# Moving four of eleven blocks of sequence 1's integer layer between the matmuls of sequence 0's down projection

## The chip, the cores and the metric

The kernel runs on one core of one Trainium2 chip. The metric is the device time of one execution in microseconds: 904.87 us, the median of three runs (904.53 to 905.12). Matmuls run on TensorE (PE in the profile), evictions and elementwise work on VectorE (DVE), ScalarE (ACT) and GpSimd (POOL); SyncE (SP) issues nearly all DMAs.

## The reference, cut to what matters

Two sequences of 512 tokens with 512 features pass four layers, each of which adds a normalised result to `x`: a state-space layer, a feed-forward layer with 4-bit integer weights ("the integer layer"), an attention over 16 head positions, and a feed-forward layer with experts ("the latent layer").

```python
x = x + _layernorm(_L0_attn_ref(_layernorm(x), ...))
x = x + _layernorm(_L0_ffn_ref(_layernorm(x), ...))    # the integer layer
x = x + _layernorm(_L1_attn_ref(_layernorm(x), ...))
x = x + _layernorm(_L1_ffn_ref(_layernorm(x), ...))
# in _L0_ffn_ref, Wg, Wu and Wd being dequantized 4-bit weights:
gate = x2 @ Wg
up = x2 @ Wu
inter = gate * jax.nn.sigmoid(gate) * up
out = (inter @ Wd).astype(jnp.float16)
```

A weight is (q - z - 1) times a scale that holds for a group of 128 rows. The inner size is 1376, cut into eleven blocks of up to 128 (`IC`); the input size of 512 is four groups.

## The kernel before, in words

The program is traced by Python generators. A stream yields after each step of matmuls; `run` (L1230) then serves one waiting request for transposes (`answer`, L1222), advances the clock of ticks (`tick`, L707) and lets every job that is due trace its next instructions. `pin` (L396) fixes the order of tracing as the order of PE, ACT, DVE and POOL. DMAs on SP are not pinned: the framework orders them, and SP issues them one after the other. `answer` serves a request no sooner than three ticks after the last one.

The state-space layer of both sequences comes first. Beside the scans of sequence 1, sequence 0 already gets its gate and up products of the integer layer, with weights that have their scales in them; its intermediate rows `it0_0` to `it0_10` then lie in SBUF.

After the scans (L1202 on) `outs` (L1285) runs 32 matmuls of sequence 1's output projection, and then sequence 0's down projection: eleven blocks times four token tiles, 44 matmuls into the four banks `fo0`. Its weights `wd0` come through the pool `wst`, three buffers, which also serves all gate and up weights. Beside that run the jobs that unpack the down weights (`words_jobs`), and `normed_job` (L1240) for each of the four token tiles of sequence 1: it normalises, asks for four transposes, and splits the result into a high and a low part, `hhl`, in float32r.

Then `run(gptq(1))` (L1635) does sequence 1's integer layer. Here the weights are plain integers (`wgi_d`), and the scales are applied when a result is evicted. `group` (L1429) multiplies one block by one group of 128 rows: two matmuls, for the high and the low part, into one of three PSUM banks (`bank`, L1214). `evict` (L1410) scales the first of a pair of groups on ACT (L1415) and adds the second to it on DVE (L1419); POOL adds the two pairs (L1423), and `inter` applies Silu on ACT and the product on DVE. A step of the stream has two groups, so a block takes four steps for gate (`fg`) and up (`fu`) together. From the third block on, each such step is followed by one down matmul (`fo`, L1394) of the block two before (`LAG = 2`), and eight down matmuls end it: 88 steps in all. The first block's weights are asked for at the start of the layer.

Beside this stream a job traces `chain(0)` (L1629) for sequence 0: eviction of `fo0` (`ffn_out`), the norm of the integer layer (`gptq_norm`), a norm with four sets of transposes (`layer_T`, tiles `tp_a`), the projection `pqkv`, the attention on DVE and ACT, and a second norm with transposes (`tp_l`). All these transposes go through one PSUM bank (`tbank`, L1209). `chain(0)` counts in the same ticks as the stream.

What follows is not pinned: `chain(1)` does the same for sequence 1 (and its `tp_a`, `pqkv` and `tp_l`), and `latent(0)` and `latent(1)` fill TensorE to the end, with `pfe`, `pup`, `pr`, `plg` and `pd`.

Of the kernel before, what the change touches and what calls it, by code (L numbers as in the profile page):

```python
# [9 lines left out]
F32 = mybir.dt.float32  # L10
F16 = mybir.dt.float16
F32R = mybir.dt.float32r
# [45 lines left out]
def tile_sandwich(  # L58
# [358 lines left out]
    with ExitStack() as mamba:  # L417
# [783 lines left out]
        ps_x = pool(ctx, "px", 1, PSUM)  # L1201
        ps_tp = pool(ctx, "ptp", 1, PSUM)  # L1202
        hlp = pool(ctx, "hl", side="right")
        hhl = [hlp.tile([P, KH, S], F32R, name=f"h{nm}1") for nm in ("hi", "lo")]

        def obank(name):
# [13 lines left out]
        answered = [0]  # L1220

        def answer():  # L1222
            if now[0] < answered[0] + 3:
                return
            answered[0] = now[0]
            fn, then = asks.pop(0)
            fn()
            spawn(then, 1)

        def run(stream, every=lambda: True):  # L1230
            for _ in stream:
# [2 lines left out]
                tick()  # L1234
                pin()

        with ExitStack() as p3:
            dq = pool(p3, "dq2", 1)

            def normed_job(i, ps):  # L1240

                name = f"mo1_{i}"
                o = new_u(f"o1_{i}")
                nc.scalar.copy(o, ps)
                yield 3
                mv = moments([o], name)
                rs = rstd(mv, name, 1)
                yield 2
                nm = minus_mean(mv, rs, name, 1)
                yield 1  # L1250
                apply(o, o, rs, nm, 0)
                yield 2
                nc.vector.tensor_add(xs(1)[i], xs(1)[i], o)
                name = f"f1_{i}"
                mv = moments([xs(1)[i]], name)
                rs = rstd(mv, name, 1)
                yield 2
                nm = minus_mean(mv, rs, name, 1)
                yield 1
                xn = jrow(f"xn_{name}")  # L1260
                apply(xn, xs(1)[i], rs, nm, 0)
                yield 2
                tps = []

                def turn():
                    tp = bank(f"tp_f1_{i}").rearrange("p (k t) -> p k t", k=KH)
                    for kc in range(KH):
                        nc.tensor.transpose(tp[:, kc, :], xn[:, ts(kc, P)], ident)
                    tps.append(tp)

                def split():
                    hi, lo = (t_[:, :, ts(i, P)] for t_ in hhl)
                    nc.scalar.copy(hi, tps[0])
                    yield 1
                    nc.vector.tensor_sub(lo, tps[0], hi.bitcast(F32))

                asks.append((turn, split()))

            def words_jobs():
                yield from down_words(0, dq, down[0])  # L1280
                yield from down_words(1, dq, down[1])
                yield 20
                yield from head_sums(dq)

            def outs():  # L1285
                po = [obank(f"po1_{i}") for i in range(TB)]
                for j in range(NCH // 2):
                    w = wo_pair(1, 0, j)
                    tiles = [(e, i) for e in range(2) for i in range(TB)]
                    for e, i in sorted(tiles, key=lambda ei: ei[j == NCH // 2 - 1]):  # L1290
                        c = 2 * j + e
                        nc.tensor.matmul(  # L1292
                            po[i], g[1][c][:, ts(i, P)], w[:, e, :],
                            start=(c == 0), stop=(c == NCH - 1),
                        )
                        yield
                        if c == NCH - 1:
                            spawn(normed_job(i, po[i]), 1)
                for i, m in enumerate(IC):
                    j, e = divmod(i, 2)  # L1300
                    if not e:
                        w = wst.tile([P, 2, H], F32, tag="w4", name=f"wd0_{j}")
                        n = len(IC[i : i + 2])
                        nc.sync.dma_start(
                            out=w[:m, :n],
                            in_=wd_d[i * P : i * P + n * m].rearrange("(k p) h -> p k h", p=m),
                        )
                    for t in range(TB):
                        if not i:
                            fo0.append(obank(f"fo0_{t}"))  # L1310
                        nc.tensor.matmul(  # L1311
                            fo0[t], its[i][:m, ts(t, P)], w[:m, e],
                            start=(i == 0), stop=(i == len(IC) - 1),
                        )
                        yield

            fo0 = []
            spawn(words_jobs(), 1)
            run(outs())
            while jobs or asks:  # L1320
                if asks:
                    answer()
                tick()
            pin()
# [17 lines left out]
        nc.sync.dma_start(out=t_[:rows], in_=src)  # L1342
        return t_

    gus16 = wdp.tile([P, 2, len(IC), KH], F16, name="gus16")
    nc.sync.dma_start(out=gus16, in_=gu_scales)
    gus = wdp.tile([P, 2, len(IC), KH], F32, name="gus")
    nc.vector.tensor_copy(gus, gus16)
    gam = wdp.tile([P, H], F32, name="gam")
    bet = wdp.tile([P, H], F32, name="bet")  # L1350

    def layer_T(b, name, ask):
# [13 lines left out]
        for i in range(TB):  # L1366
            while i >= 2 and i - 2 not in done_tp:
                yield 1
            xn = nrow(f"xn_{name}{b}_{i}")
            apply(xn, xs(b)[i], rs, nm, i)  # L1370
            yield 1

            def turn(i=i, xn=xn):
                tp = done_tp[i] = tbank(f"tp_{name}{b}_{i}").rearrange("p (k t) -> p k t", k=KH)
                for kc in range(KH):
                    nc.tensor.transpose(tp[:, kc, :], xn[:, ts(kc, P)], ident)  # L1376

            def out(i=i):
                nc.scalar.copy(hT[:, :, ts(i, P)], done_tp[i])
                done.append(i)  # L1380
                yield 1

            ask(turn, out())
# [2 lines left out]

    def gptq(b):
        fo = [obank(f"fo{b}_{t}") for t in range(TB)]
        its, ups, parts = {}, {}, {}

        def down(i, w):
            m = IC[i]
            for t in range(TB):
                nc.tensor.matmul(  # L1394
                    fo[t], its[i][:m, ts(t, P)], w[:m],
                    start=(i == 0), stop=(i == len(IC) - 1),
                )
                yield
# [2 lines left out]
            m = IC[i]  # L1401
            return w2(wd_d[i * P : i * P + m, :], f"wd{b}_{i}", m)

        def inter(i):
            m, it, up = IC[i], its[i], ups[i]
            nc.scalar.activation(it[:m], it[:m], AF.Silu)
            yield 1
            nc.vector.tensor_mul(it[:m], it[:m], up[:m])

        def evict(a, i, k, ps):  # L1410
            m = IC[i]
            sc = gus[:m, a, i, k : k + 1]
            if k % 2 == 0:
                t_ = parts[a, i, k] = row(f"p{'gu'[a]}{b}_{i}_{k}")
                nc.scalar.activation(t_[:m], ps[:m], AF.Copy, scale=sc)  # L1415
                return
            t_ = parts[a, i, k - 1]
            yield 1
            nc.vector.scalar_tensor_tensor(t_[:m], ps[:m], sc, t_[:m], ALU.mult, ALU.add)  # L1419
            if k == KH - 1:  # L1420
                yield 1
                p0 = parts[a, i, 0]
                nc.gpsimd.tensor_add(p0[:m], p0[:m], t_[:m])  # L1423
                (ups if a else its)[i] = p0
                if a:
                    yield 2
                    yield from inter(i)

        def group(a, i, k, w):  # L1429
            e, m = i % 2, IC[i]  # L1430
            ps = bank(f"f{'gu'[a]}{b}_{i}_{k}")
            for n, part in enumerate(hhl):
                nc.tensor.matmul(  # L1433
                    ps[:m], w[:, k, e * P : e * P + m].bitcast(F32R), part[:, k, :],
                    start=(n == 0), stop=(n == 1),
                )
            spawn(evict(a, i, k, ps), 1)

        LAG = 2
        wd = {}  # L1440
        for i in range(len(IC)):
            if i % 2 == 0:
                ws = gu_weights(b, i // 2)
            wd[i] = wd_load(i)
            dn = down(i - LAG, wd[i - LAG]) if i >= LAG else iter(())
            for a in range(2):
                for k in range(0, KH, 2):
                    group(a, i, k, ws[a])
                    group(a, i, k + 1, ws[a])
                    yield  # L1450
                    for _ in dn:
                        yield
                        break
        for i in range(len(IC) - LAG, len(IC)):
            yield from down(i, wd[i])
        fos[b] = fo

    fos = {}
# [255 lines left out]
```

## Time and profile before

| | |
|---|---|
| median of three runs | 904.87 us (904.53 to 905.12) |
| profiled execution, its own time | 905.83 us |
| span of the profile, first to last instruction | 904.1 us |
| mean granted TensorE clock over the span | 0.971 |
| sequence 0's down projection begins | 599.55 us |
| integer layer of sequence 1 | 639.54 to 735.41 us |
| `latent(0)` begins | 735.41 us |
| last matmul ends, about | 894.25 us |

In a profile's list by time, a row gives the start and the length in us, engine, line and operation, `out<-in`, the shapes and the count, and in brackets how long the engine had idled before it and what released it. In a table of busy time by stage, a row gives the stretch and its length, the busy time and count for PE, PEld (the loading of weights into TensorE), DVE, ACT and POOL, the granted clock of TensorE, the share of the DMA engines that was busy, and GB/s. In the groups, a row gives the line, engine and operation, the shapes and the count, then the busy time, the mean length in ns, and the idle time before with its releaser. A matmul of float32 shows as two passes, one of float32r as one.

### The profile page before, as it was taken

The page shows a single profiled execution, that of the slowest core. Times are in us where ns is not written, and L with a number is a line of the kernel's source. Part 1 is how long each engine was busy: PE and PEld are TensorE (multiplying, and loading weights), DVE is VectorE, ACT ScalarE, POOL GpSimd, SP SyncE. Part 2 cuts the span into 40 slices and gives each one's busy share as a digit, 9 for nine tenths or more (in the row PEclk, how much of TensorE's full clock was granted, in tenths as well). Part 3 has the DMA queues.
Part 4 walks back from the last instruction along what each step waited for, and adds up shares of the span by engine and source line. Part 5 has one row for each costly group of instructions (what it writes and reads, how often), then busy time and mean ns, then how long its engine had stood idle before and what let it go on. Part 6 is the DMA issues. An engine that isn't in the chain of part 4 may idle for free. (4 is left out here: it accounts for less than half of the span.)

```text
span 904.1 us, 7390 instructions
## 1 busy us (share of the span) xinstructions
PE 826.8 (91%) x2188; PEld 382.6 (42%) x2188; DVE 717.8 (79%) x835; ACT 441.1 (49%) x682; POOL 507.0 (56%) x354
## 2 busy tenths in 40 slices
PE   6889979797999989779999998999989999999995
PEld 3434434233454434334444442344456545545442
DVE  5869999999999999999999998763576964444226
ACT  3359875657666755566566653031455444400110
POOL 6767796778778878876787878540233410011001
PEclk9998999898999999979999999799999999999998
DMA  6759211110001765300011112572322331101001
GB/s 214 283 205 381 80 55 56 47 55 31 24 1 61 259 252 196 107 0 24 24 46 47 32 33 78 187 252 81 93 71 82 95 106 47 46 12 58 24 0 47
DMA packets 47418, 85.76 MB, mean 95 GB/s; under 512 B 8302, under 2 KB 22489, under 8 KB 47378
## 3 DMA queue, kind: packets, MB, share of 16 engines
q1 hardware_dynamic: 45106, 79.30, 25.8%
q0 software_dynamic: 1984, 5.47, 1.7%
q10 hardware_dynamic: 288, 0.52, 0.2%
q8 instruction: 17, 0.28, 0.1%
q14 instruction: 23, 0.19, 0.1%
HBM read 68.40 MB, written 16.88 MB: 94 GB/s over the span
## 5 line engine op out<-in xcount | busy, mean ns | idle before, releaser
L1100 POOL TENSOR_TENSOR bx<-bx,C 128x1024 f32<-128x1024 f32 x128 | 302.3, 2362 | 101.9 <-DVE bx L1094 79.7
L1094 DVE TENSOR_TENSOR_SCAN bx<-da,bx 128x1024 f32<-128x1024 f32 x128 | 292.3, 2283 | 0.5 <-ACT da L1074 0.4
L1122 PE MATMUL py<-bx,ident 128*128 128x512 f32 x480 | 234.9, 619 | 27.9 <-POOL bx L1100 24.3
L1074 ACT ACTIVATE da<-dt,A 128x511 f32<-128x511 f32 x256 | 176.9, 692 | 149.4 <-DVE bx L1094 144.7
L1122 PEld LDWEIGHTS py<-bx,ident 128*128 128x128 f32 x480 | 91.6, 196 | 153.1 <-issue 97.1
L1090 DVE TENSOR_TENSOR bx<-du,B 128x1024 f32<-128x1024 f32 x127 | 153.4, 1209 | 2.3 <-DMA B<-scr 0.3
L130 POOL TENSOR_TENSOR rs_lo<-ve_lo,mhalf 128x1 f32<-128x1 f32 x8 | 7.1, 882 | 91.8 <-DVE ve_lo L128 91.8
L745 PE MATMUL pg<-xT,w_g 128*128 128x512 f32 x114 | 55.8, 620 | 1.1 <-ACT dt L563 1.1
L1554 PE MATMUL pup<-hT_l,wup 128*128 128x512 f32 x128 | 56.2, 593 | 0.0
L1618 PE MATMUL pd<-wdn,hid 128*128 128x512 f32 x128 | 55.5, 594 | 0.0
L1423 POOL TENSOR_TENSOR pg<-pg,pg 128x512 f32<-128x512 f32 (+1 forms) x11 | 15.3, 1392 | 59.2 <-DVE pg L1419 59.2
L1394 PE MATMUL fo<-wd,pg 128*128 128x512 f32 (+1 forms) x88 | 44.2, 593 | 0.1
L1014 PE MATMUL fg<-hT_f,wg 128*128 128x512 f32 (+1 forms) x88 | 42.5, 594 | 0.0
L1014 PE MATMUL fu<-hT_f,wu 128*128 128x512 f32 (+1 forms) x88 | 40.4, 594 | 1.4 <-ACT dt L563 1.4
L475 DVE SCALAR_TENSOR_TENSOR u<-px,ch,u 128x511 f32<-128x511 f32 (+2 forms) x48 | 35.9, 747 | 6.5 <-ACT u L468 5.4
L1311 PE MATMUL fo<-wd,it 128*128 128x512 f32 (+1 forms) x88 | 38.6, 592 | 0.0
L1618 PEld LDWEIGHTS pd<-wdn,hid 128*128 128x128 f32 x128 | 24.6, 192 | 31.2 <-issue 30.7
L1571 DVE TENSOR_TENSOR hid<-hid 128x512 f32<-128x512 f32 x16 | 11.0, 688 | 32.0 <-ACT hid L1570 31.8
L1554 PEld LDWEIGHTS pup<-hT_l,wup 128*128 128x128 f32 x128 | 23.9, 190 | 28.2 <-issue 28.2
L745 PEld LDWEIGHTS pg<-xT,w_g 128*128 128x128 f32 x114 | 22.1, 198 | 31.6 <-issue 28.7
L1419 DVE SCALAR_TENSOR_TENSOR pg<-fg,gus,pg 128x512 f32<-128x512 f32 (+1 forms) x22 | 16.4, 744 | 21.5 <-ACT pg L1415 21.5
L615 PE MATMUL px<-xT,w_x 128*128 128x512 f32 x64 | 31.7, 645 | 0.7 <-ACT xT L595 0.7
(253 smaller groups left out, 1256.5 us busy)
## 6 DMA issues: line engine op xcount, KB each, us to landing
wo<-in_W_outT SPq DMA_DIRECT2D x20, 512.0 KB
B<-scr SPq DMA_DIRECT2D x16, 512.0 KB
C<-scr SPq DMA_DIRECT2D x16, 512.0 KB
w_x<-in_W_in SPq DMA_DIRECT2D x8, 512.0 KB
wgi_d<-q_gu SPq DMA_DIRECT2D x16, 256.0 KB
wgu_d<-w_gu POOLq DMA_DIRECT2D x16, 256.0 KB, 2.6
w_g<-in_W_in SPq DMA_DIRECT2D x8, 512.0 KB
wup<-in_up_w SPq DMA_DIRECT2D x8, 512.0 KB
```

Of the source, the lines that this page charges most:

```text
L475: nc.vector.scalar_tensor_tensor(uc[:, s:], ps[:, : S - s], ch[:, c, KCONV - 1 - s : KCONV - s], uc[:, s:], ALU.mult, ALU.add,)
L745: nc.tensor.matmul(ps, w[:, k, ts(e, P)], xT[b][:, k, :], start=(k == 0), stop=(k == KH - 1))
L1014: nc.tensor.matmul(ps[:m], wt[j][a][:, kc, e * P : e * P + m], hT[:, kc, :], start=(kc == 0), stop=(kc == KH - 1),)
L1074: nc.scalar.activation(das[s % 2][:, i, 1:], st["dt", b, c][:, 1:], AF.Exp, scale=A[:, c, n : n + 1])
L1090: nc.vector.tensor_mul(bx, st["du"].unsqueeze(1).to_broadcast([P, NG, S]), Bbs[b][gi])
L1094: nc.vector.tensor_tensor_scan(flat, das[s % 2].rearrange("p n t -> p (n t)"), flat, 0.0, ALU.mult, ALU.add)
L1100: nc.gpsimd.tensor_mul(bxs[s], bxs[s], Cbs[b][s % NGI])
L1122: nc.tensor.matmul(st["y"], ident, bx[:, i, :], start=False, stop=last)
L1311: nc.tensor.matmul(fo0[t], its[i][:m, ts(t, P)], w[:m, e], start=(i == 0), stop=(i == len(IC) - 1),)
L1394: nc.tensor.matmul(fo[t], its[i][:m, ts(t, P)], w[:m], start=(i == 0), stop=(i == len(IC) - 1),)
L1554: nc.tensor.matmul(ps, w[:, kc, ts(e, P)], src[kc], start=(kc == 0), stop=(kc == KH - 1))
L1618: nc.tensor.matmul(pd, hid[kc][:, ts(i, P)], wdn[kc], start=(kc == 0), stop=(kc == INT // P - 1),)
```

## The change

Blocks 0 to 3 (`MIX = 4`) of sequence 1's integer layer move into the stretch of sequence 0's down projection. `mixed` runs down matmuls until all four tiles of `hhl` are split, and then one step of two groups for every two down matmuls. The gate rows of the four blocks get their own pool (`it1`), other partial rows reuse `g1` tiles. `wd0` gets its own three buffers, and the scales `gus` are loaded earlier. All jobs are drained before `gptq` begins.

`gptq` has the other seven blocks: four steps of groups alone (`FIRST = 4`), then one step of groups and one down matmul by turns (`GD = 2`). `downs` now starts with block 0, without a lag. When the groups are at their end, their turns pass as ticks without a matmul. `answer` may serve a request at every tick, and of sequence 0's sets of transposes every second one uses `bank` instead of `tbank`.

```diff
         hlp = pool(ctx, "hl", side="right")
+        gus16 = hlp.tile([P, 2, len(IC), KH], F16, name="gus16")
+        nc.sync.dma_start(out=gus16, in_=gu_scales)
+        gus = hlp.tile([P, 2, len(IC), KH], F32, name="gus")
+        nc.vector.tensor_copy(gus, gus16)
...
-            if now[0] < answered[0] + 3:
+            if now[0] < answered[0] + 1:
                 return
...
+        def int_groups(row, a, i, ws):
+
+            for k in range(0, KH, 2):
+                group(a, i, k, ws[a], row)
+                group(a, i, k + 1, ws[a], row)
+                yield
+
+        def int_layer(row, i0, i1):
+
+            for i in range(i0, i1):
+                if i % 2 == 0 or i == i0:
+                    int_ws[0] = gu_weights(1, i // 2)
+                for a in range(2):
+                    yield from int_groups(row, a, i, int_ws[0])
+
+        its1, ups, parts, int_ws, ready = {}, {}, {}, [None], set()
+        MIX, GD, FIRST = 4, 2, 4
+
+        itp = pool(ctx, "it1", MIX, side="right")
         with ExitStack() as p3:
             dq = pool(p3, "dq2", 1)
+            wdq = pool(p3, "wd0", 3, side="right")
...
+            def down0():
                 for i, m in enumerate(IC):
                     j, e = divmod(i, 2)
                     if not e:
-                        w = wst.tile([P, 2, H], F32, tag="w4", name=f"wd0_{j}")
+                        w = wdq.tile([P, 2, H], F32, tag="wd0", name=f"wd0_{j}")
...
+            def row1(a, i, k):
+                if (a, k) == (0, 0):
+                    return itp.tile([P, S], F32, tag="it", name=f"it1_{i}")
+                row1s[0] += 1
+                return g1_tile(F32, row1s[0] % NCH, f"p{'gu'[a]}1_{i}_{k}")
+
+            row1s = [-1]
+
+            def mixed():
+                fo = down0()
+                while split_count[0] < TB:
+                    next(fo)
+                    yield
+                gu = int_layer(row1, 0, MIX)
+                ends, n = {}, 0
+                while not all(ends.get(k) for k in (gu, fo)):
+                    k = fo if n % 3 else gu
+                    ends[k] = next(k, True)
+                    n += 1
+                    yield
...
             run(outs())
+            run(mixed())
             while jobs or asks:
                 if asks:
                     answer()
                 tick()
...
-                tp = done_tp[i] = tbank(f"tp_{name}{b}_{i}").rearrange("p (k t) -> p k t", k=KH)
+                tp = done_tp[i] = (tbank if b or i % 2 == 0 else bank)(f"tp_{name}{b}_{i}").rearrange("p (k t) -> p k t", k=KH)
...
+        def downs():
+            wd = {0: wd_load(0), 1: wd_load(1)}
+            for i in range(len(IC)):
+                if i + 2 < len(IC):
+                    wd[i + 2] = wd_load(i + 2)
+                while i not in ready:
+                    yield "wait"
+                yield from down(i, wd.pop(i))
+
+        gu, dn = int_layer(row_, MIX, len(IC)), downs()
+        for _ in range(FIRST):
+            next(gu)
+            yield
+        n, gu_end, dn_end = 0, None, None
+        while not (gu_end and dn_end):
+            if n % GD == 0:
+                gu_end = next(gu, True)
+            else:
+                dn_end = next(dn, True)
+                if dn_end == "wait":
+                    gu_end, dn_end = next(gu, True), None
+            n += 1
+            yield
```

`group`, `evict` and `inter` move out of `gptq` to be used by both stretches, with the tile that receives a partial result given by `row`; they trace the same instructions as before.

More of the change, by code (lines that the diff above doesn't have):

```diff
@@ L1235, in run, with inter, evict, group @@
                 pin()
+        def inter(i):
+            m, it, up = IC[i], its1[i], ups.pop(i)
+            nc.scalar.activation(it[:m], it[:m], AF.Silu)
+            yield 1
+            nc.vector.tensor_mul(it[:m], it[:m], up[:m])
+            ready.add(i)
+        def evict(a, i, k, ps, row):
+            m = IC[i]
+            sc = gus[:m, a, i, k : k + 1]
+            if k % 2 == 0:
+                t_ = parts[a, i, k] = row(a, i, k)
+                nc.scalar.activation(t_[:m], ps[:m], AF.Copy, scale=sc)
+                return
+            t_ = parts[a, i, k - 1]
+            yield 1
+            nc.vector.scalar_tensor_tensor(t_[:m], ps[:m], sc, t_[:m], ALU.mult, ALU.add)
+            if k == KH - 1:
+                yield 1
+                p0 = parts[a, i, 0]
+                nc.gpsimd.tensor_add(p0[:m], p0[:m], t_[:m])
+                (ups if a else its1)[i] = p0
+                if a:
+                    yield 2
+                    yield from inter(i)
+        def group(a, i, k, w, row):
+            e, m = i % 2, IC[i]
+            ps = bank(f"f{'gu'[a]}1_{i}_{k}")
+            for n, part in enumerate(hhl):
+                nc.tensor.matmul(
+                    ps[:m], w[:, k, e * P : e * P + m].bitcast(F32R), part[:, k, :],
+                    start=(n == 0), stop=(n == 1),
+                )
+            spawn(evict(a, i, k, ps, row), 1)
+        def int_groups(row, a, i, ws):
[12 more added lines that the diff above has]
+        itp = pool(ctx, "it1", MIX, side="right")
         with ExitStack() as p3:
             dq = pool(p3, "dq2", 1)
+            wdq = pool(p3, "wd0", 3, side="right")
             def normed_job(i, ps):
@@ L1275, in split @@
                     nc.vector.tensor_sub(lo, tps[0], hi.bitcast(F32))
+                    split_count[0] += 1
                 asks.append((turn, split()))
@@ L1315, in outs @@
                         yield
-            fo0 = []
+            def row1(a, i, k):
[16 more added lines that the diff above has]
+                    yield
+            fo0, split_count = [], [0]
             spawn(words_jobs(), 1)
             run(outs())
+            run(mixed())
             while jobs or asks:
@@ L1343, in w2 @@
         return t_
[L1345 to L1348, printed above, removed]
     gam = wdp.tile([P, H], F32, name="gam")
@@ L1388, in gptq @@
         fo = [obank(f"fo{b}_{t}") for t in range(TB)]
-        its, ups, parts = {}, {}, {}
         def down(i, w):
@@ L1394, in down @@
                 nc.tensor.matmul(
-                    fo[t], its[i][:m, ts(t, P)], w[:m],
+                    fo[t], its1[i][:m, ts(t, P)], w[:m],
                     start=(i == 0), stop=(i == len(IC) - 1),
@@ L1402, in wd_load @@
             return w2(wd_d[i * P : i * P + m, :], f"wd{b}_{i}", m)
[L1404 to L1453, printed above, removed]
@@ L1454, in gptq, with row_ @@
-        for i in range(len(IC) - LAG, len(IC)):
-            yield from down(i, wd[i])
+        def row_(a, i, k):
+            return row(f"p{'gu'[a]}1_{i}_{k}")
+        def downs():
[7 more added lines that the diff above has]
+        gu, dn = int_layer(row_, MIX, len(IC)), downs()
```

## The prediction

> **What bounds the kernel now.** I read the page first, then the matmuls in order of time from 599 us, busy time by stage, the waits, and the groups by form. The page says that TensorE is the busy engine to the end, and that from slice 24 it seldom rests:
>
> ```profile
> PE 826.8 (91%) x2188; PEld 382.6 (42%) x2188; DVE 717.8 (79%) x835; ACT 441.1 (49%) x682; POOL 507.0 (56%) x354
> ...
> PE   6889979797999989779999998999989999999995
> ```
>
> So a change that only reorders matmuls can win only what TensorE idles in the stretch concerned. That stretch begins with sequence 0's down projection at 599.55. Timeline of TensorE:
>
> ```profile
> 599.98 7.89 PE L1311 MATMUL fo<-wd,it 128*128 128x512 f32 x18
> 607.71 0.60 PE L1268 MATMUL tp_f<-ident,xn_f 128*128 128x128 f32 x4
> ...
> 617.19 22.48 PE L1311 MATMUL fo<-wd,it 128*128 128x512 f32 x52
> ...
> 735.41 7.13 PE L1554 MATMUL pfe<-hT_l,wfe 128*128 128x512 f32 x16
> ```
>
> 52 passes fill 617.19 to 639.54: 0.43 us a pass, 0.86 a down matmul (two passes), nothing lost. In the integer layer a *unit* is two groups, four matmuls. Unit plus down matmul recur every 1.79 us (690.30, 692.09, 693.88), so a unit is 0.93. A set of four transposes takes 0.44 (610.72 to the next matmul at 611.16), the attention projection 3.5 (685.34 to 688.83). Busy time by stage gives the elapsed times:
>
> ```profile
> 639.54:651.79 12.25, 10.62 (x38) 5.78 (x36) 9.93 (x23) 9.12 (x14) 4.93 (x4) 1.00 0.38 103
> 651.79:671.33 19.54, 18.02 (x57) 10.15 (x57) 18.43 (x31) 7.42 (x12) 7.50 (x6) 1.00 0.31 98
> 671.33:685.34 14.01, 13.15 (x53) 8.26 (x53) 6.11 (x9) 9.62 (x16) 3.83 (x3) 1.00 0.21 57
> 685.34:735.41 50.07, 49.30 (x185) 29.66 (x183) 37.73 (x65) 28.12 (x44) 17.53 (x13) 1.00 0.32 96
> ```
>
> Elapsed minus work is what TensorE lost. First row: 9 units, 8.4 of work, lost 3.85. Second: 9 units and 10 downs, 17.0, lost 2.5. Third: 6 units, 6 downs, four sets of transposes, 12.5, lost 1.5. Fourth: 20 units, 28 downs, projection, four sets, 48.0, lost 2.0. Together 9.85 us, and no more can be won here. The cause stands in the groups by form (DVE's and ACT's evictions, 0.74 and 0.69 us each) and in the wait of a unit: it starts when an eviction frees its PSUM bank.
>
> ```profile
> L1419 DVE SCALAR_TENSOR_TENSOR pg<-fg,gus,pg 128x512 f32<-128x512 f32 x20 | 14.9, 744 | 21.5 <-ACT pg L1415 21.5
> ...
> L1415 ACT ACTIVATE pg<-fg,gus 128x512 f32<-128x512 f32 x20 | 13.7, 687 | 18.2 <-PE fg L1433 18.2
> ...
> 665.70 0.50 PE L1433 MATMUL fu<-hhi,wu 128*128 128x512 f32 x1 [0.81 <-DVE pg L1419]
> ```
>
> **The change part by part.** The order on each compute engine is the order of tracing, so I count ticks (one per step of the matmul stream). The count is tested on before: it puts the first tp_a set behind 10 downs and the first tp_l set behind 35, as the trace has them.
>
> *Scales.* One load and a cast (0.20) move from 619.84 to ahead of the nibbles at 570.39. Were the load late, the down words slip; their cover is the wd0 load issued at 591.66 for a use at 599.55. I take 0 (bounds 0 and +2); past the cover each us costs one. On SP, the load waited 10.8 us for py; that wait goes, and nothing behind it was late.
>
> *Loads.* wd0 gets three buffers of its own, so wg and wu of the first pairs no longer wait for them (before: issued 629.40, 636.27, 639.70). Six wd0 and four wgi loads of 512 KB in some 70 us are 75 GB/s; the slices at 600 to 610 moved over 380. I take 0; the price of a late one is under the rivals.
>
> *Transposes.* Asks of sequence 1's norm come two ticks apart. The old spacing of 3 put sets at 607.71, 610.72, 613.74, 616.75; now 607.71 plus 0.44 + 1.72 each: 609.87, 612.03, 614.18. The rows xn_f end at 605.60, 608.23, 610.85, 613.48, in time. The last split follows by the old latency (set 616.75, hlo done 618.70: 1.95), so 616.13; TensorE, with one down behind the set, wants its first unit at 615.48. Lost: 0.7.
>
> *Mixed stretch.* 16 downs are done, 28 remain for 16 units: unit, down, down, 2.65 us. An eviction pair is 0.69 on ACT and 0.74 on DVE, so banks are long free; 0.2 lost (the downs end after 14 units, the last two units touch). Silu's table load (1.28) goes here too, hidden.
>
> *Start of the second stretch.* Before it all jobs are drained, so block 3's last product stands on DVE ahead of the next evictions. It waits for DVE 0.75, then POOL's add 1.3, after the last group ends (time 0): it is done at 3.2, and unit 2's first groups pass while unit 1's second group is evicted only at 3.85. Unit 3 needs that bank and could start at 2.06: it waits 1.85. With 0.35 for bank latency elsewhere, 2.2 lost, in place of 3.85.
>
> *Ticks 5 to 33.* From tick 9 units, downs and the norm of sequence 0 lie as in before, so 2.5 stays. The tp_a sets come one tick apart, and odd ones take a unit's bank; ACT carries 8.8 us there (four xn, four copies, four evictions, two Silu) beside 8.9 on TensorE. I take 1.4 (before 1.5; bounds 0.5 and 3).
>
> *Attention beside units.* Nine units are left after the projection; 0.7, as before up to the same point (704.8).
>
> *The last transposes.* Here something new waits. Units end at tick 51; from then a down comes every second tick, and the tp_l sets are written at ticks 71 to 74, behind 19 downs and 9 units after the projection: 16.3 + 8.4 + 0.7 = 25.4 us. The attention behind them is no faster: the first DVE step of its closing norm (ao) starts 15.7 after the projection (704.51), and from there sequence 1's run, with little beside it, took 11.7 (768.45 to 780.16). I add 1.2 for nm_ao (1.24 us in before beside a POOL add, 0.16 in sequence 1) and take off 0.3 for products of the other sequence: 28.35. TensorE is in order; 11 downs stand behind the set, and it idles 2.95, plus 0.25 for the fourth set's xn. Bounds 1 and 4.5.
>
> ```profile
> 747.69 0.66 PE L1376 MATMUL tp_a<-ident,xn_a 128*128 128x128 f32 x4 [1.72 <-ACT xn_a L153]
> ...
> 780.16 0.66 PE L1376 MATMUL tp_l<-ident,xn_l 128*128 128x128 f32 x4 [0.99 <-ACT xn_l L153]
> ...
> 562.86 2.60 PE L1122 MATMUL py<-bx,ident 128*128 128x512 f32 x4 [2.39 <-POOL bx L1100]
> 565.97 3.78 PE L1122 MATMUL py<-bx,ident 128*128 128x512 f32 x4 [0.51 <-POOL bx L1100]
> ...
> 789.08 3.49 PE L1585 MATMUL pr<-wf,exo 128*128 128x512 f32 x4
> ```
>
> *The clock.* A gap of 1.72 left the clock alone. Gaps of 0.83, 2.39 and 0.51 within 8 us were followed by passes of 0.85 (565.97), eight of them, 3.4 us lost, at a granted 0.50; 3.6 us of tiny plg matmuls by four of 0.82, 1.6 lost. My 2.95 is nearest the second gap, so I count a drop, at the smaller price, 1.6 (bounds 0 and 3.4). [...] No run here shows a gap of 2.95 by itself.
>
> **Sum.** Lost after: 0.7 + 0.2 + 2.2 + 2.5 + 1.4 + 0.7 + 3.2 = 10.9, against 9.85, or +1.1; the matmuls are the same. With the clock it is +2.7. The profiled execution took 905.83 (span 904.10), 0.96 over the median; the difference carries over: 904.87 + 2.7 = 907.6.
>
> **The rivals.** *The clock stays up:* +1.1, 906.0, not slower by the 0.2% (1.8 us) that a measurement here can tell. It decides if the tp_l gap counts as too short; for it speaks 747.69, against it 562.86. *Evictions ease:* 16 of 44 units leave the stretch that shares DVE and ACT with sequence 0's norm. If the loss went by units, 9.85 x 28/44 = 6.3, plus 0.9 ahead, and the tp_l wait vanished in the freed DVE time, it is 7.2, so 902.2. Against it: the second and third rows' losses lie in ticks whose order stays. *A late load:* SP issues in order; two wd0 loads held it 7.2 us (615.71). With a wgi load behind such a wait, up to 7 us of TensorE idles: about 913. For it: the new order of SP is unknown; against it: all releases follow TensorE's order.
>
> **How the numbers follow.** Forecast 0.38, clock up 0.30, evictions ease 0.17, late load 0.15. The range runs from 902.5, the easing rival's near side, to 911.5 (forecast with the other bounds: 1.3 more at tp_l, 1.8 more clock, and some of a late load). Faster 0.20 (easing and a little of the second), same 0.28, slower 0.52.
>
> **What would show it.** Transposes tp_f near 609.9, 612.0, 614.2; the first unit at 616.2 with under 1 us idle; units every 2.65 us to about 655; an idle of some 1.8 us two units later behind a DVE eviction; an idle near 3 us ahead of the first tp_l, with ACT's xn_l as releaser, and passes of 0.85 behind it; the latent layer's start about 2.7 later than 735.41. I am wrong if units in the second stretch run without bank waits, if the tp_l set finds xn_l ready, or if TensorE waits for a DMA.

## The result and the profile after

The changed kernel takes 908.87 us, the median of ten runs (906.08 to 913.28), against 904.99 us for the kernel before in the same rounds (903.86 to 906.30). The ratio is 1.0048 with a 95% interval of 1.0028 to 1.0068: slower by 2.5 to 6.2 us. The profiled execution took 908.44 us, with a span of 906.6 us and a mean granted clock of 0.971, the same clock as before.

TensorE's busy time and the slices in which it rests, from the page of the changed kernel:

```profile
PE 824.8 (91%) x2188; PEld 382.3 (42%) x2188; DVE 714.6 (79%) x835; ACT 440.6 (49%) x682; POOL 507.8 (56%) x354
...
PE   6988979797999989879999998999989899999995
...
PEclk9998999898999999979999999999999999998998
```

The work is the same, and the page shows little: from slice 24 on a single digit differs from before, the eight in slice 32 (703 to 725 us), where a nine stood. TensorE's timeline (start, length, operation, and in brackets the idle time ahead and its releaser) shows more:

```profile
570.17 27.70 PE L1353 MATMUL po<-wo,g 128*128 128x512 f32 x64 [0.83 <-issue]
597.72 7.89 PE L1373 MATMUL fo<-wd,it 128*128 128x512 f32 x18
605.44 0.60 PE L1328 MATMUL tp_f<-ident,xn_f 128*128 128x128 f32 x4
...
607.93 0.66 PE L1328 MATMUL tp_f<-ident,xn_f 128*128 128x128 f32 x4 [0.17 <-ACT xn_f L153]
...
610.55 0.66 PE L1328 MATMUL tp_f<-ident,xn_f 128*128 128x128 f32 x4 [0.25 <-ACT xn_f L153]
...
615.56 0.50 PE L1271 MATMUL fg<-hlo,wg 128*128 128x512 f32 x1 [0.56 <-DVE hlo L1335]
...
616.36 1.88 PE L1373 MATMUL fo<-wd,it 128*128 128x512 f32 x4
...
619.01 1.88 PE L1373 MATMUL fo<-wd,it 128*128 128x512 f32 x4
...
658.50 0.50 PE L1271 MATMUL fu<-hhi,wu 128*128 128x512 f32 x1 [1.28 <-DVE pg L1257]
...
668.59 0.50 PE L1271 MATMUL fg<-hhi,wg 128*128 128x512 f32 x1 [0.36 <-DVE pu L1257]
...
673.21 0.50 PE L1271 MATMUL fu<-hhi,wu 128*128 128x512 f32 x1 [0.77 <-DVE pg L1257]
...
714.28 8.74 PE L1472 MATMUL fo<-wd,pg 128*128 128x512 f32 x20
726.29 0.65 PE L1456 MATMUL tp_l<-ident,xn_l 128*128 128x128 f32 x4 [3.26 <-ACT xn_l L153]
...
737.90 7.03 PE L1606 MATMUL pfe<-hT_l,wfe 128*128 128x512 f32 x16
```

The mixed stretch runs as it was meant to: a unit and two down matmuls every 2.65 us (616.36, 619.01), and nothing lost. Behind it units wait for banks that DVE's evictions free, first 1.28 us and then five times 0.20 to 0.77 up to 682.60 (two of the five are shown), and then comes one idle of 3.26 us, the longest of the whole stretch: TensorE has run ten down matmuls (twenty passes) ahead of the first `tp_l` set and stands at it, because the rows `xn_l` are not there. In before the same set has no bracket, and `po` took 1.87 us longer:

```profile
570.58 29.57 PE L1292 MATMUL po<-wo,g 128*128 128x512 f32 x64 [0.83 <-issue]
...
724.74 0.60 PE L1376 MATMUL tp_l<-ident,xn_l 128*128 128x128 f32 x4
```

Busy time by stage (stretch and length; then PE, PEld, DVE, ACT, POOL; granted clock, DMA share, GB/s), for the mixed stretch, for the drain with the first five units behind it, and for the units up to the first `tp_a` set:

```profile
616.36:654.55 38.19, 38.19 (x117) 21.69 (x115) 14.13 (x20) 13.40 (x20) 8.94 (x7) 1.00 0.22 65
654.55:661.84 7.29, 5.84 (x21) 3.48 (x21) 4.73 (x9) 5.45 (x11) 2.58 (x2) 1.00 0.26 74
661.84:686.27 24.43, 22.13 (x69) 12.13 (x68) 23.49 (x46) 9.73 (x16) 10.49 (x8) 1.00 0.29 86
```

In the first row TensorE is busy for all of 38.19 us and DVE for 14.13. In the third DVE is busy for 23.49 of 24.43 us, 96%, and all five waits there end with its evictions: I read this as DVE setting the time there, not TensorE. The second row of before that the prediction shows has a like figure, 18.43 of 19.54, 94%.

From here on two stretches measure the kernels: **S**, from the first `po` matmul to the first `pfe` matmul, which holds everything that the change touches, and its part **T**, from the first `fo` of sequence 0 to `pfe`. All times are starts on TensorE's timeline.

| kernel | `po` starts | `fo` starts | `pfe` starts | S | T | measured time over before's, us (95%) |
|---|---|---|---|---|---|---|
| before | 570.58 | 599.98 | 735.41 | 164.83 | 135.43 | |
| before, again | 566.82 | 594.37 | 731.68 | 164.86 | 137.31 | |
| after | 570.17 | 597.72 | 737.90 | 167.73 | 140.18 | +3.9 (+2.5 to +6.2) |
| after, again | 573.14 | 600.68 | 743.09 | 169.95 | 142.41 | |
| `late_tpl` | 570.70 | 600.14 | 735.28 | 164.58 | 135.14 | +1.2 (-1.4 to +2.7) |
| `tail4` | 566.76 | 594.30 | 733.87 | 167.11 | 139.57 | +3.6 (+1.9 to +5.6) |
| `both` | 568.83 | 596.37 | 731.26 | 162.43 | 134.89 | -3.5 (-4.7 to -0.3) |
| `mix0` | 568.76 | 596.31 | 733.75 | 164.99 | 137.44 | +0.6 (-0.3 to +3.6) |
| `six_blocks` | 571.79 | 601.22 | 737.38 | 165.59 | 136.16 | -1.5 (-3.7 to +0.6) |
| `six_fast` | 569.25 | 598.67 | 729.27 | 160.02 | 130.60 | -5.6 (-6.3 to -2.6) |
| `spacing3` | 569.85 | 597.39 | 744.24 | 174.39 | 146.85 | |

The last column is the difference of the medians; its interval is that of the ratio times 905 us (the ratio is not the quotient of the medians, so it may sit off the middle). Behind `pfe` all kernels but the two with six blocks run the same order (from `pfe` to the first `plg` run 50.08 to 50.13 us in all nine traces), and differ behind that by the clock, in the steps that the last section gives.

### The profile page after: what moved, and what is told of

Same layout as the page of the kernel before. It is cut to its first block, busy times and chain, and to the rows that moved or that the text cites. A ratio compares the mean times of both kernels' runs of the same rounds, so it can differ in the third digit from the quotient of the medians.

```text
span 906.6 us, 7385 instructions
## 1 busy us (share of the span) xinstructions
PE 824.8 (91%) x2188; PEld 382.3 (42%) x2188; DVE 714.6 (79%) x835; ACT 440.6 (49%) x682; POOL 507.8 (56%) x354
## 5 line engine op out<-in xcount | busy, mean ns | idle before, releaser
L1373 PE MATMUL fo<-wd,it 128*128 128x512 f32 (+1 forms) x88 | 40.9, 592 | 0.0
L1261 POOL TENSOR_TENSOR pu<-pu,pu 128x512 f32<-128x512 f32 (+1 forms) x11 | 16.0, 1450 | 35.3 <-DVE pu L1257 35.3
L615 PE MATMUL px<-xT,w_x 128*128 128x512 f32 x64 | 32.0, 648 | 0.7 <-ACT xT L595 0.7
L983 PE MATMUL po<-wo,g 128*128 128x512 f32 x64 | 30.7, 618 | 0.9 <-DMA wo<-in_W_outT 0.9
L745 PE MATMUL px<-xT,w_x 128*128 128x512 f32 x64 | 29.8, 595 | 1.0 <-ACT xT L839 1.0
```

What stands on the lines that cost most here:

```text
L615: nc.tensor.matmul(ps, w[:, k, ts(c % 2, P)], xT[0][:, k, :], start=(k == 0), stop=(k == KH - 1))
L745: nc.tensor.matmul(ps, w[:, k, ts(e, P)], xT[b][:, k, :], start=(k == 0), stop=(k == KH - 1))
L1373: nc.tensor.matmul(fo0[t], its[i][:m, ts(t, P)], w[:m, e], start=(i == 0), stop=(i == len(IC) - 1),)
```

## The experiments

### One idle: the first `tp_l` set, traced later

`layer_T` writes the `tp_l` sets of sequence 0 ten ticks later, so that more down matmuls stand ahead of them:

```diff
         done, done_tp = [], {}
+        if name == "l" and not b:
+            yield 10
         for i in range(TB):
```

> The changed kernel, with ten more ticks between sequence 0's second norm and its tp_l transposes, so that five more down matmuls stand ahead of them. Theory (TensorE, in order, idles 3.3 us ahead of the first tp_l set while downs that could run stand behind it): the idle vanishes, five downs take 4.3 us of it, and the time falls by about 3.3 us, to about 905.5. Rival 1 (sequence 0's chain is simply late, and the latent layer would wait for it instead): the idle moves to the start of pfe, no gain, 908 to 909. Rival 2 (the spread of the changed kernel, 906 to 913, comes from a clock that drops in this gap in some executions): the fall is larger, 4 to 5 us, and the spread shrinks to about 2 us.

Measured: 905.86 us against 904.66 before, ratio 1.0007 (0.9985 to 1.0030). TensorE's timeline of this kernel at the same place:

```profile
715.15 13.04 PE L1474 MATMUL fo<-wd,pg 128*128 128x512 f32 x30
728.02 0.60 PE L1458 MATMUL tp_l<-ident,xn_l 128*128 128x128 f32 x4
...
735.28 7.03 PE L1608 MATMUL pfe<-hT_l,wfe 128*128 128x512 f32 x16
```

Fifteen down matmuls now stand ahead of the set, the bracket is gone, and from the projection to `pfe` it takes 40.59 us in place of 44.08: 3.5 less. That is the idle of 3.26 and the short wait at a later set. With it nothing is left of the slowdown that can be told from no change. The runs are still spread over 900.3 to 907.7 us, so the spread does not come from this gap alone; before's own runs beside them spread over 900.3 to 910.5 us.

### The other idle: the drain

The order of the mixed stretch is changed so that units come more often, and the down matmuls, not the units, are its end. The last products then find TensorE at work:

```diff
-                    k = fo if n % 3 else gu
+                    k = gu if n % 5 in (0, 3) else fo
```

> The changed kernel, with the mixed stretch as two units to three downs, so that the units end four downs early. Theory (the wait of the second stretch's third unit comes from block 3's last product, which stands on DVE ahead of the evictions because all jobs are drained first): the downs at the end cover the product, the 1.3 us idle and the waits around it go, 1.5 to 2 us less, about 907. Rival (the first units are slowed by the ACT copies of fo0 and the bn_stats of sequence 0's norm): the same time as the changed kernel, the wait stays.

Measured: 908.30 us, ratio 1.0041 (1.0021 to 1.0062). The wait of 1.28 us is gone, and the time from the first unit to `tp_a` falls from 71.76 to 69.87 us, 1.9 less, as expected. But the first wait that is left, and the row of the stage behind it, are those of after:

```profile
663.33 0.50 PE L1271 MATMUL fg<-hhi,wg 128*128 128x512 f32 x1 [0.36 <-DVE pu L1257]
...
667.96 0.50 PE L1271 MATMUL fu<-hhi,wu 128*128 128x512 f32 x1 [0.79 <-DVE pg L1257]
```

```profile
656.59:681.04 24.45, 22.14 (x70) 12.16 (x68) 23.49 (x46) 9.73 (x16) 10.51 (x8) 1.00 0.29 86
721.03:733.87 12.84, 12.84 (x39) 6.85 (x40) 1.69 (x5) 5.95 (x10) 0.00 (x0) 0.87 0.17 42
```

So the drain costs 1.9 us, and the bank waits behind it stay: that stage keeps its length to 0.02 us (24.45 against 24.43). In time the gain can't be told from none. The second row says part of why for the profiled execution: the same idle of 3.25 us ahead of `tp_l` was here followed by a granted clock of 0.87 over the stretch, in after by 1.00, which costs 1.2 us.

What the drain is can be read on DVE's timeline in after:

```profile
657.10 0.69 DVE L1245 TENSOR_TENSOR it<-it,pu 128x512 f32<-128x512 f32 x1 [1.46 <-POOL pu L1261]
657.71 1.40 DVE L1257 SCALAR_TENSOR_TENSOR pg<-fg,gus,pg 128x512 f32<-128x512 f32 x2
```

Block 3's last product stands ahead of the next evictions in DVE's order and waits 1.46 us for POOL's sum; two evictions run right behind it, and the unit at 658.50 waits for the first.

### The same two kernels once more

No edit: one more execution of each, to see what of the clock belongs to the kernel.

> The changed kernel unchanged, a second profile. Theory (clock gate): if the execution takes 910 or more, the profile shows passes of 0.85 us either after the scans (near 566 to 574) or behind the idle ahead of tp_l (near 726); if it takes 907 or less, in neither place. Rival: the extra time of slow executions lies in waits for DMAs, at a granted clock of 1.0.

> The kernel before unchanged, a second profile. Theory: the stretch from the first down matmul of sequence 0 to pfe takes 135.4 us again, and passes of 0.85 us after the scans (near 566 to 574) are there again, since the times of this kernel hardly spread (903.9 to 906.3). Rival: the half clock after the scans is chance, and without it the time is some 2 us lower.

After again took 915.27 us, and as the expectation has it for 910 or more, there are passes at half clock. The idle ahead of `tp_l` is the same to 0.01 us, but now the passes behind it run at half clock (two passes of a down matmul in 1.92 us in place of 1.02):

```profile
728.86 1.12 PE L1456 MATMUL tp_l<-ident,xn_l 128*128 128x128 f32 x4 [3.26 <-ACT xn_l L153]
729.76 1.92 PE L1472 MATMUL fo<-wd,pg 128*128 128x512 f32 x2
731.47 1.91 PE L1456 MATMUL tp_l<-ident,xn_l 128*128 128x128 f32 x8
```

From the set to `pfe` it takes 14.23 us in place of 11.61, 2.6 more. Of the 6.8 us over after's profiled execution, 3.0 lie ahead of `po`, 2.2 in S and 1.6 behind the start of `pfe`.

Before again took 902.13 us. The half clock that before had at the start of `po` is not there (64 passes in 27.70 us, where before needed 29.57):

```profile
560.70 5.29 PE L1122 MATMUL py<-bx,ident 128*128 128x512 f32 x8 [2.39 <-POOL bx L1100]
566.82 27.70 PE L1292 MATMUL po<-wo,g 128*128 128x512 f32 x64 [0.83 <-issue]
```

Instead the clock fell at the attention projection (0.85, 0.50 and 0.79 in the three slices of 2 us from 682 to 688 us, 1.6 us lost), so that S is the same, 164.86. What the expectation said of passes of 0.85 there and of T (137.31, not 135.4) fell. Its rival stood in part: whether the half clock behind the scans lasts into `po` differs by execution, but S does not shrink with it. The 3.70 us between the two executions of before lie ahead of `po`, which starts 3.76 us earlier; 1.6 of them come behind the idle of 2.39 us, where before runs at half clock for longer, and the rest was not traced.

### Both idles at once

The edits of the first two together.

> The changed kernel with both edits of the first two runs (tp_l ten ticks later; units end four downs early). Theory (each idle is TensorE's own loss, and the two do not overlap): the gains add, 3.3 + 1.9 = 5.2 us less than the changed kernel, about 903.5, and the stretch from the start of sequence 1's output projection to pfe is 5.2 us shorter than the changed kernel's 167.7. Rival (the chain of sequence 0 is the bound, so what is won ahead of it is lost at its end): no more than late_tpl alone, 905.5 to 906, with TensorE waiting at pfe.

Measured: 901.96 us against 905.44, ratio 0.9973 (0.9948 to 0.9997). S is 162.43, 5.3 less than in after; 3.5 and 1.9 make 5.4. The two gains add, so the two idles are separate causes, and together they are more than the whole slowdown. The bank waits of 0.36, 0.76, 0.20, 0.67 and 0.21 us between 665 and 680 us are still there.

### Nothing moved: the rest of the change alone

No block is multiplied between sequence 0's down matmuls; all eleven stay beside their own. All else of the change stays.

```diff
-        MIX, GD, FIRST = 4, 2, 4
+        MIX, GD, FIRST = 0, 2, 4
-        itp = pool(ctx, "it1", MIX, side="right")
+        itp = pool(ctx, "it1", 1, side="right")
```

> The changed kernel with no block moved (all eleven in the second stretch; everything else of the change stays). Theory (the tp_l wait exists because units end early, and the drain's wait because units precede the drain): neither wait is there, units are left until the last ticks, and the loss is some 8 to 9 us, so 903 to 905, no slower than the kernel before. Rival (the slowdown comes from the other parts of the change: spacing of the requests, the shared banks, the order of loads): the time stays at 907 to 909.

Measured: 906.06 us, ratio 1.0019 (0.9997 to 1.0040), between the two expectations and not to be told from before. TensorE's timeline, the `tp_l` set and two of eight bank waits between 642 and 663 us:

```profile
655.88 0.50 PE L1271 MATMUL fg<-hhi,wg 128*128 128x512 f32 x1 [0.27 <-DVE pu L1257]
...
663.02 0.50 PE L1271 MATMUL fu<-hhi,wu 128*128 128x512 f32 x1 [0.81 <-DVE pg L1257]
...
716.35 0.60 PE L1456 MATMUL tp_l<-ident,xn_l 128*128 128x128 f32 x4
```

The idle ahead of `tp_l` is made by the move: with all units still to do beside the chain of sequence 0, there is work enough ahead of the set. The bank waits are not made by the move. S is 164.99, that of before. T is 2 us longer than before's, which a faster `po` (27.55 us) makes up; 0.5 of it are two `tp_f` waits of 0.25, the rest was not taken apart.

### The transposes three ticks apart again

```diff
-            if now[0] < answered[0] + 1:
+            if now[0] < answered[0] + 3:
```

> The changed kernel with requests served no sooner than every third tick again. Theory (from tick 51 on ticks cost TensorE only half a down, so what the chain has still to do then decides): the tp_f waits (0.7 us) go, but the attention stands 7 ticks further back when the units end; tp_l comes behind 3 more downs (2.6 us) while its data come some 6 us later relative to the units' end, so the idle ahead of tp_l grows from 3.3 to between 5 and 7 us. Rival (more room between requests gives the data time): the idle ahead of tp_l shrinks below 2 us.

One profiled run: 913.05 us. TensorE's timeline:

```profile
692.26 0.50 PE L1271 MATMUL fu<-hhi,wu 128*128 128x512 f32 x1 [1.20 <-ACT pg L1253]
...
700.83 3.71 PE L1531 MATMUL pqkv<-w,hT_a 128*128 128x48 f32 x32
```

The sets of `tp_a` come further apart, and the projection starts 15.10 us behind the first in place of 7.55. Sequence 0's chain falls further behind the units and downs, so the idle ahead of `tp_l` grows, to 4.35 us, under the 5 to 7 that were expected, but in that direction; there are further waits for ACT, and half clock behind the gap (two passes of a down matmul in 1.92 us in place of 1.02). That `answer` serves each tick is a part of the change that pays: without it S was 6.7 us longer in this execution, the clock included.

### More units moved, and DVE relieved

Six blocks move, one step of groups for one down matmul. For sequence 1's own down projection three blocks' worth of steps are left beside the norm, at one step of groups for two downs; the turns left over at the end count twice in ticks.

```diff
-        MIX, GD, FIRST = 4, 2, 4
+        MIX, GD, FIRST = 6, 3, 2
-                    k = fo if n % 3 else gu
+                    k = fo if n % 2 else gu
             yield
+            if gu_end:
+                yield
```

> Six blocks moved instead of four, one unit to one down in the mixed stretch (units end four downs early), two units alone at the start of the second stretch and then two downs to a unit, two ticks a step after the units' end. Theory (units beside sequence 0's down projection lose nothing, and units beside its norm and attention lose 0.1 to 0.4 us each to evictions that wait for DVE): the loss falls from about 14 us to 5 to 7, the time to 900 to 902, below the kernel before. Rival (with fewer units in the second stretch the chain of sequence 0 is too slow, and TensorE waits for tp_a, pqkv or tp_l): the bank waits go and waits for xn_a or xn_l of 3 to 6 us come, 904 to 907.

Measured: 903.95 us, ratio 0.9983 (0.9959 to 1.0007), not the 900 to 902 of the theory. The rows of the units beside the norm, and of the end of the stretch:

```profile
666.95:688.98 22.03, 22.03 (x67) 12.46 (x66) 19.66 (x43) 7.86 (x13) 7.92 (x7) 1.00 0.25 72
726.00:737.38 11.38, 7.26 (x22) 4.95 (x23) 3.29 (x11) 6.24 (x10) 1.01 (x1) 0.56 0.01 1
```

DVE is at 89% in place of 96, and TensorE is busy for all of the 22.03 us: the bank waits are gone. This fits the reading that DVE set the time there, though the edit also gives that stretch one unit for two downs in place of one for one. But the last row has a granted clock of 0.56 and 4 us of idle:

```profile
723.85 1.12 PE L1472 MATMUL fo<-wd,pg 96*128 96x512 f32 x2 [1.28 <-DVE pg L1245]
730.12 1.97 PE L1456 MATMUL tp_l<-ident,xn_l 128*128 128x128 f32 x8 [5.15 <-ACT xn_l L153]
```

With the units gone earlier, the chain through attention is longer than the work beside it, by 5.15 us. This is the rival that the expectation named.

So the last kernel keeps the six blocks and shortens that chain by removing eight ticks that it spent waiting for its turn, and spends them ahead of the `tp_l` sets, which so keep their place among the downs:

```diff
+        if name == "l" and not b:
+            yield 8
         for i in range(TB):
...
-        yield 2
+        yield 1
         mx = lp.tile([P, TB, HD], F32, tag="mx", name=f"mx{b}")
         nc.vector.tensor_reduce(mx, sc, AX.X, ALU.max)
-        yield 2
+        yield 1
...
-        yield 3
+        yield 2
         o = lp.tile([P, TB, HD], F32, tag="ao", name=f"ao{b}")
         nc.vector.tensor_reduce(o, sc, AX.X, ALU.add)
-        yield 3
+        yield 2
...
             nc.vector.tensor_add(xv, xv, o[:, i, :].unsqueeze(2).to_broadcast([P, HD, NH]))
-            yield 2
+            yield 1
```

> Six blocks moved as in six_blocks, with sequence 0's attention traced eight ticks faster and those eight ticks put ahead of its second set of transposes, so that tp_l keeps its place among the downs. Theory (in six_blocks the attention was held back by the ticks its steps were given, not by the engines): the 5.2 us idle ahead of tp_l falls below 1.5, with it the half clock behind it (some 2 us), and the time to 898 to 900. Rival (DVE is full there): units wait for banks as long as tp_l did before, 902 to 905, no gain over six_blocks.

Measured: 899.91 us (897.47 to 904.87) against 905.55, ratio 0.9950 (0.9930 to 0.9971): faster than before, and than after, which stood at 1.0048 of before; the theory's 898 to 900 held. The same views:

```profile
664.40:686.43 22.03, 22.03 (x68) 12.46 (x66) 19.64 (x43) 7.87 (x13) 7.93 (x7) 1.00 0.27 74
721.27:729.27 8.00, 7.15 (x24) 4.26 (x25) 1.40 (x4) 6.41 (x11) 0.82 (x1) 0.79 0.10 29
```

```profile
721.27 1.12 PE L1474 MATMUL fo<-wd,pg 96*128 96x512 f32 x2 [1.25 <-DVE pg L1245]
723.25 1.97 PE L1458 MATMUL tp_l<-ident,xn_l 128*128 128x128 f32 x8 [0.85 <-ACT xn_l L153]
...
729.27 7.03 PE L1610 MATMUL pfe<-hT_l,wfe 128*128 128x512 f32 x16
```

The wait for `xn_l` is 0.85 in place of 5.15 us. The half clock behind it was expected to go; it is shorter but there (0.79 over that row). S is 160.02, 4.8 us less than before; the measured gain is 2.6 to 6.3 us. How much the shorter chain wins with fewer blocks moved, or none, was not run.

## Why the prediction was right, and where its steps were not

The forecast of 907.6 us and its sign held: 908.87, slower by 0.48%, in the range. Its main step did as well: the idle ahead of `tp_l`, which before does not have, is the longest idle and the largest loss that the change adds. But the terms did not all hold, and the total owes something to chance.

- **Loads.** Held. No matmul between 597 and 738 us waits for a DMA; the late-load rival fell. One reading was off: before moved 314 GB/s from 600 to 605 us, and over 380 (392) only from 605 to 610.
- **Transposes, 0.7.** Missed by 1.5. From the first `fo` (597.72) to 616.36, 16 downs, four sets and a unit are 16.45 us of work and took 18.64: 2.2 lost. The last split was foreseen: the first unit lost 0.9 (0.56 of it a wait for `hlo`). The rows `xn_f` "in time" were not: waits of 0.17, 0.25 and 0.25 us stand in the brackets, and around each set 0.2 more is lost. The prediction took their times from an execution in which `po` ran at half clock at first, 29.4 us. In after it ran at full clock, 27.55, and TensorE came to the sets earlier than the norm. Where `po` took 29.4 us again (`late_tpl`, `six_blocks`, `six_fast`) the sets stand 2.16 us apart with no wait, as worked out.
- **Mixed stretch, 0.2.** Held: 38.19 us busy of 38.19 up to 654.55.
- **Start of the second stretch, 2.2.** Held, 2.6 (7.29 us for 4.65 us of units); the removed cause is worth 1.9 in `tail4`. The unit waited 1.28 us by its bracket, where 1.85 was said (the two times from which the prediction takes it, 3.85 and 2.06, make 1.79).
- **Ticks 5 to 33, "so 2.5 stays".** This is the step whose mechanism failed. Twelve downs and eleven units are 20.55 us of work and took 24.43: 3.9 lost. The prediction counted that the drain takes the place of a loss of 3.85 and the rest stays. But from the start of the units to `tp_a` DVE has the same 28 us of work before and after (28.36 and 28.22). Before lost 6.4 us there in 31.8, after 6.5 in 31.7. I read the loss as a debt of DVE: what isn't paid in the first ticks is paid later. The 94% of the second row stood in the prediction's own view and was not read; it read the length of an eviction instead. `tail4` supports the reading: there DVE has three operations fewer in this stretch (650.65 to 681.04), its work falls by 1.4 us to 26.80, and the stretch by 1.3 to 30.39. In before, after, `tail4` and `both` the stretch is DVE's busy time plus 3.4 to 3.6 us. `six_blocks`, with DVE at 89%, lost nothing there, which supports it too; DVE's operations alone were not shortened in any run.
- **`tp_a` 1.4, attention 0.7.** Held: 1.3 and 0.85.
- **The last transposes, 2.95 + 0.25.** Held: 3.26 + 0.15, and another 0.4 in the downs behind. (The prediction's terms for the data, 15.7, 11.7, 1.2 and -0.3, make 28.3, not 28.35.) `late_tpl` took 3.5 us off, and `mix0` shows that the move makes it.
- **The clock, 1.6.** Neither right nor wrong: the same gap cost 0 in after, 1.2 in `tail4` and 2.6 in after again. Behind idles of 3.25 and 3.26 us the granted clock over the stretch up to `pfe` was 0.87 in `tail4`, 0.79 in after again and 1.00 in after, so passes at half clock followed in two of three executions. Whether a gap of 2.95 us leaves the clock alone, no run shows.

**How the total came out.** The sum was +1.1 without the clock. T of the profiled execution grew by 4.75 us, the terms above: 2.2 + 0.15 + 2.6 + 3.9 + 1.3 + 0.85 + 3.8 = 14.8 lost, where 9.85 were before; the 0.2 us between is rounding of the work. Against it `po` ran 1.85 us faster by its clock, and began 0.4 earlier; so `pfe` starts 2.5 us later, near the predicted 2.7 for another reason. The medians differ by 3.9; S grew by 2.9 in one pair of profiles and 5.1 in the other.

Of the rivals, "the clock stays up" is what the profiled execution did, yet not at its 906.0; "evictions ease" fell: with 16 units in place of 18 ahead of `tp_a`, but the same DVE work, as much was lost there.

## What to carry to other kernels

Where an in-order engine runs two chains in one written order, count for the last step of the slower chain how much work stands ahead of it and how much behind: moving work out of that stretch to fill a place elsewhere takes away the cover, and the idle appears at the next step of the slow chain, here 3.26 us for a move that lost nothing where it put the work. Read the second engine's share in a stage before counting its instructions one by one: here TensorE lost 2.5 to 3.9 us where DVE was busy for 94 to 96%, and nothing at 89%. With the same 28 us of DVE work the two kernels lost 6.4 and 6.5 us, only in different places. Both idles had small remedies of order (a later place for the waiting step, another end for the mixed stretch), and with more moved and the chain shortened the same idea wins 0.5%.

## What the runs showed of the hardware that was not expected

The granted clock turns the same program into several times, in steps. The latent layer's part between the two `plg` runs has the same instructions in all kernels; it took 32.89 us in after, `tail4`, `six_fast` and `spacing3`, 34.5 in before, before again, `late_tpl`, `mix0` and `six_blocks`, and 36.2 in after again and `both`. The part behind it took 74.1 us in nine traces, and 75.8 in after and `tail4`. The steps are 1.65 to 1.7 us, what 3.3 us at half clock loses. Before shows one: its clock was 0.84, 0.50 and 0.80 in the three slices of 2 us from 788 to 794 us, which loses 1.7 us, and after's was 1.00 there. The ten times of after lie up to 7 us apart, and the clock behind the start of `po` is not all of that: the two executions of before, 3.70 us apart, agree in S to 0.03 us and differ ahead of it.

The length of one gap does not decide alone. In `six_fast` idles of 1.25 and 0.85 us, 2 us apart, were followed by 0.50 in the slice from 724 to 726 us, and the short gaps at the end of the scans (0.83 and 2.39 us) are followed by a slice of 2 us at 0.50 to 0.56 in every trace; a lone gap of 3.26 us left the clock at 1.00 in after. In before again the clock fell to 0.50 in the slice from 684 to 686 us, behind the 32 small matmuls of the attention projection, with no idle in brackets between 673 and 682 us. What decides beside that length was not settled by these runs.
